# Second layer of a four-layer graph network: when K is put in place, when the bound is taken, and when the first tile of adj is fetched

## Chip, cores and metric

The kernel runs on one core of one Trainium2 chip. The metric is the device time of one execution in microseconds (us), median of several runs. One core has five engines with a queue of instructions each: TensorE (PE, matmuls), VectorE (DVE), ScalarE (ACT), GpSimd (POOL) and SyncE (SP). DMA transfers between SBUF, the on-chip memory, and DRAM are issued from the queues of SP, ACT and POOL. All sizes are float32.

## What is computed

Four graph layers run one after the other on x (4096 x 128) with one adjacency matrix adj (4096 x 4096, zeros and ones, symmetric); each is followed by a residual and a layer norm. The change touches the second one, a transformer convolution with 4 heads of 32 channels:

```python
def _transformer_conv(x, adj, Wq, bq, Wk, bk, Wv, bv, Ws, bs, Wb):
    q = (x @ Wq + bq).reshape(n, H, C)
    k = (x @ Wk + bk).reshape(n, H, C)
    v = (x @ Wv + bv).reshape(n, H, C)
    attn = jnp.einsum('nhc,mhc->hnm', q, k) / np.float32(np.sqrt(C))
    mask = adj == 0.0
    # softmax of attn over m where mask is false, called alpha
    out = jnp.einsum('hnm,mhc->hnc', alpha, v)
    out = jnp.transpose(out, (1, 2, 0)).reshape(n, C * H)
    x_r = x @ Ws + bs
    beta = jax.nn.sigmoid(jnp.concatenate([out, x_r, out - x_r], axis=-1) @ Wb)
    return beta * x_r + (1.0 - beta) * out
```

## The kernel before

The second layer has a prologue and a loop. The prologue computes q and k in 8 chunks of S = 512 nodes. Each chunk is cut into a rounded part and a remainder (`cut`), written to the DRAM tensor `qk`, and read back by `stack` into an arrangement in which one 128-row matmul gives the sum of the partial products of one head: `KS` holds all of k (4096 nodes), `QS[0]` and `QS[1]` hold one chunk of q each. The prologue also computes v (into `VA`) and x_r (written to the DRAM tensor `rd`), and a bound on the scores: if it is at most SAFE, the exponential needs no shift.

```python
KS = keep.tile([P, NH, N], F32R, tag="KS", name="KS")
QS = [keep.tile([P, NH, S], F32R, tag=f"QS{k}", name=f"QS{k}") for k in range(2)]
# ...
def stack(a, dst, c):                       # four transfers of 32 partitions
    for r, part in enumerate(((0, 1, 0, 1), (0, 0, 1, 1))[a]):
        nc.gpsimd.dma_start(
            out=dst[r * C : (r + 1) * C, :, :],
            in_=qk[a, part, :, c * S : (c + 1) * S].rearrange("(h c) n -> c h n", h=NH),
        )
# ...
for c in range(NC):                         # NC = 8
    s = slice(c * S, (c + 1) * S)
    for a, w, bias in ((1, wk, bkc), (0, wq, bqc)):
        p = self.ps_t.tile([P, S], F32, tag="pt", name="pqk")
        nc.tensor.matmul(p, lhsT=w, rhs=XT[:, s], start=True, stop=True)
        cut = rot.tile([P, 2, S], F32R, tag="cut", name="cut", bufs=4)
        nc.scalar.activation(cut[:, 0, :], p, AF.Identity, bias=bias)             # L820
        nc.vector.scalar_tensor_tensor(cut[:, 1, :], p, bias, ...)                # L821
        nc.vector.tensor_reduce(mx[:, a, c : c + 1], ..., ALU.max, ...)           # L824
        nc.sync.dma_start(out=qk[a, :, :, s].rearrange("k p n -> p k n"), in_=cut.bitcast(F32))
        if a:
            stack(1, KS[:, :, s], c)
        elif c < 2:
            stack(0, QS[c], c)
# the bound: m2 from mx, one matmul pb, a reduction, then fi = (bound <= SAFE)    # L833 to L843
for g in self.groups():                     # 8 groups of 4: v                    # L844
    # ... 4 matmuls pt <- XT, wv; 4 additions V[:, t, :, 0:C] = p + bvr           # L847, L849
for g in self.groups():                     # 8 groups of 4: x_r                  # L855
    # ... 4 matmuls pt <- XT, ws                                                  # L858
    r = rot.tile([P, 4, D], F32, tag="r", name="r")       # rot has 2 buffers
    nc.vector.tensor_tensor(r, p, bsr..., ALU.add)                                # L860
    nc.sync.dma_start(out=rd[:, g[0] : g[-1] + 1, :], in_=r)

small = nc.values_load(fi, min_val=0, max_val=1)
with tc.If(small > 0) as cmp:
    self.attention_unshifted(VA, KS, QS, stack, rd, wb)
with cmp.Else():
    self.attention_shifted(V, qk, rd, wb)
```

The loop (`attention_unshifted`, the branch that runs with these inputs) has 8 tiles I of 512 nodes with 32 steps jb each. A step forms the scores of 4 heads (`ps`), their exponentials (`e`), masks them with a piece of the transposed adj (`at`), and, two steps later, multiplies them into the sums (`pv`). Inside it the instructions keep the order in which they are written.

```python
atp = ctx.enter_context(tc.tile_pool(name="atf", bufs=2))
def load(I, J):                             # 1 MB of adjT, on SP's queue
    at = atp.tile([P, 4, S], F32, tag="at", name="at")
    nc.sync.dma_start(out=at, in_=self.adjT[I, J])                                # L884
    st["at", I, J] = at
# row(n): 1 MB of adj into nat, on ACT's queue (L894); degree(n): ACT sums nat (L901), then row(n + 1)
# scores(I, jb): ps <- KS, QS (L909); e = exp(ps) (L916); e *= (at != 0) (L918)
# sums(I, jb): pv <- VA, e (L935)

nc.scalar.preload_act_table_set("natural_log_exp_and_others")                     # L1006
load(0, 0)
load(0, 1)
row(0)
for n in range(-LEAD, len(seq)):            # LEAD = 2
    if n + LEAD < len(seq):
        I, jb = seq[n + LEAD]
        if jb % 4 == 0:
            m = n + LEAD + 4
            if m < len(seq) and (m // 4) > 1:
                load(m // NT, m % NT // 4)
        if jb % 4 == 3:
            degree(8 * I + jb // 4)
        if jb == 3 and 0 < I < NS - 1:
            stack(0, QS[(I + 1) % 2], I + 1)
        scores(I, jb)
    if n >= 0:
        sums(*seq[n])
        # ... and the ending of the tile before, in pieces
```

Of the kernel before, what the change touches and what calls it, by code (L numbers as in the profile page):

```python
# [16 lines left out]
P = 128  # L17
# [7 lines left out]
S = 512  # L25
# [5 lines left out]
class Net:  # L31
# [737 lines left out]
    def layer1(self, Wq, bq, Wk, bk, Wv, bv, Ws, bs, Wb):  # L769


        nc, tc, N, NT, D, X = self.nc, self.tc, self.N, self.NT, self.D, self.X
        NH, C = 4, D // 4
        with ExitStack() as ctx:
            self.on_scalar = 4
            keep = ctx.enter_context(tc.tile_pool(name="keep1", bufs=1))

            VA = keep.tile([P, NT * NH * (C + 1) + 32], F32, tag="VA", name="VA")
            V = VA[:, 0 : NT * NH * (C + 1)].rearrange("p (t h c) -> p t h c", t=NT, h=NH)
            KS = keep.tile([P, NH, N], F32R, tag="KS", name="KS")  # L780
            QS = [keep.tile([P, NH, S], F32R, tag=f"QS{k}", name=f"QS{k}") for k in range(2)]

            qk = self.dram.tile([2, 2, P, N], F32, tag="qk", name="qk")
            rd = self.dram.tile([P, NT, D], F32, tag="rd", name="rd")
            wb = [self.load_row(Wb[k * D : (k + 1) * D, 0], f"wb{k}") for k in range(3)]

            nc.vector.tensor_tensor(wb[0], wb[0], wb[2], ALU.add)
            nc.vector.tensor_tensor(wb[1], wb[1], wb[2], ALU.subtract)
            fi = self.const.tile([1, 1], mybir.dt.int32, tag="fi", name="fi")
            wq, wk = self.load_mat(Wq, "wq"), self.load_mat(Wk, "wk")  # L790
            wv, ws = self.load_mat(Wv, "wv"), self.load_mat(Ws, "ws")
            bqc, bkc = self.load_col(bq, "bqc"), self.load_col(bk, "bkc")
            bvr, bsr = self.load_row(bv, "bvr"), self.load_row(bs, "bsr")

            def stack(a, dst, c):
# [7 lines that stand above are left out]
            with ExitStack() as pctx:  # L803
                pre = pctx.enter_context(tc.tile_pool(name="pre1", bufs=1))
                rot = pctx.enter_context(tc.tile_pool(name="rot1", bufs=2))
                self.ps_t = pctx.enter_context(tc.tile_pool(name="ps_t", bufs=8, space=PSUM))
                nc.gpsimd.memset(VA, 1.0)
                XT = pre.tile([P, N], F32, tag="XT", name="XT")
                NC = N // S
                mx = pre.tile([P, 2, NC], F32, tag="mx", name="mx")  # L810
                self.transposed(X, XT)
                nc.vector.tensor_scalar(bqc, bqc, 1.0 / math.sqrt(C), None, op0=ALU.mult)
                nc.vector.tensor_scalar(wq, wq, 1.0 / math.sqrt(C), None, op0=ALU.mult)
                for c in range(NC):
                    s = slice(c * S, (c + 1) * S)
                    for a, w, bias in ((1, wk, bkc), (0, wq, bqc)):
                        p = self.ps_t.tile([P, S], F32, tag="pt", name="pqk")
                        nc.tensor.matmul(p, lhsT=w, rhs=XT[:, s], start=True, stop=True)
                        cut = rot.tile([P, 2, S], F32R, tag="cut", name="cut", bufs=4)
                        nc.scalar.activation(cut[:, 0, :], p, AF.Identity, bias=bias)  # L820
                        nc.vector.scalar_tensor_tensor(  # L821
                            cut[:, 1, :], p, bias, cut[:, 0, :].bitcast(F32), op0=ALU.add, op1=ALU.subtract
                        )
                        nc.vector.tensor_reduce(  # L824
                            mx[:, a, c : c + 1], cut[:, 0, :].bitcast(F32), AX.X, ALU.max, apply_absolute_value=True
                        )
                        nc.sync.dma_start(out=qk[a, :, :, s].rearrange("k p n -> p k n"), in_=cut.bitcast(F32))
                        if a:
                            stack(1, KS[:, :, s], c)
                        elif c < 2:  # L830
                            stack(0, QS[c], c)

                m2 = pre.tile([P, 2], F32, tag="m2", name="m2")  # L833
                nc.vector.tensor_reduce(m2, mx, AX.X, ALU.max)
                nc.vector.tensor_tensor(m2[:, 0:1], m2[:, 0:1], m2[:, 1:2], ALU.mult)
                hd = pre.tile([P, NH], F32, tag="hd", name="hd")
                nc.gpsimd.memset(hd, 0.0)
                for h in range(NH):
                    nc.gpsimd.memset(hd[h * C : (h + 1) * C, h : h + 1], 1.0)
                p = self.ps_t.tile([P, S], F32, tag="pt", name="pb")  # L840
                nc.tensor.matmul(p[0:1, 0:NH], lhsT=m2[:, 0:1], rhs=hd, start=True, stop=True)
                nc.vector.tensor_reduce(m2[0:1, 0:1], p[0:1, 0:NH], AX.X, ALU.max)
                nc.vector.tensor_scalar(fi, m2[0:1, 0:1], SAFE, None, op0=ALU.is_le)  # L843
                for g in self.groups():  # L844
                    p = self.ps_t.tile([P, 4, P], F32, tag="pt", name="pt")
                    for k, t in enumerate(g):
                        nc.tensor.matmul(p[:, k, :], lhsT=XT[:, t * P : (t + 1) * P], rhs=wv, start=True, stop=True)  # L847
                    for k, t in enumerate(g):
                        nc.vector.tensor_tensor(  # L849
                            V[:, t, :, 0:C],  # L850
                            p[:, k, :].rearrange("p (h c) -> p h c", h=NH),
                            bvr.rearrange("p (h c) -> p h c", h=NH),
                            ALU.add,
                        )
                for g in self.groups():  # L855
                    p = self.ps_t.tile([P, 4, P], F32, tag="pt", name="pt")
                    for k, t in enumerate(g):
                        nc.tensor.matmul(p[:, k, :], lhsT=XT[:, t * P : (t + 1) * P], rhs=ws, start=True, stop=True)  # L858
                    r = rot.tile([P, 4, D], F32, tag="r", name="r")
                    nc.vector.tensor_tensor(r, p, bsr.unsqueeze(1).to_broadcast([P, 4, D]), ALU.add)  # L860
                    nc.sync.dma_start(out=rd[:, g[0] : g[-1] + 1, :], in_=r)

            small = nc.values_load(fi, min_val=0, max_val=1)
            with tc.If(small > 0) as cmp:
                self.attention_unshifted(VA, KS, QS, stack, rd, wb)
            with cmp.Else():
                self.attention_shifted(V, qk, rd, wb)

    def attention_unshifted(self, VA, KS, QS, stack, rd, wb):

        nc, tc, N, NT, NS, D, X = self.nc, self.tc, self.N, self.NT, self.NS, self.D, self.X
        NH, C = 4, D // 4
# [1 line left out]
        with ExitStack() as ctx:  # L874
# [2 lines left out]
            ep = ctx.enter_context(tc.tile_pool(name="ef", bufs=3))  # L877
            ps_s = ctx.enter_context(tc.tile_pool(name="ps_s", bufs=3, space=PSUM))
            ps_v = ctx.enter_context(tc.tile_pool(name="ps_v", bufs=1, space=PSUM))
            st = {}  # L880

            def load(I, J):
                at = atp.tile([P, 4, S], F32, tag="at", name="at")
# [120 lines left out]
            rest = iter(())  # L1004
            with tc.manual_schedule():
                nc.scalar.preload_act_table_set("natural_log_exp_and_others")  # L1006
                load(0, 0)
                load(0, 1)
                row(0)
                for n in range(-LEAD, len(seq)):  # L1010
# [5 lines that stand above are left out]
                                load(m // NT, m % NT // 4)  # L1016
                        if jb % 4 == 3:
                            degree(8 * I + jb // 4)
                        if jb == 3 and 0 < I < NS - 1:
                            stack(0, QS[(I + 1) % 2], I + 1)  # L1020
                        scores(I, jb)
                    if n >= 0:
                        I, jb = seq[n]
                        sums(I, jb)
                        next(rest, None)
                        if jb == NT - 1:
                            for _ in rest:
                                pass
                            rest = ending(I)
                            next(rest)  # L1030
# [416 lines left out]
```

## Time and profile before

| | |
|---|---|
| time, median of 3 runs | 2433.75 us (2432.07 to 2436.35) |
| span of the profiled execution | 2429.7 us |
| mean granted TensorE clock | 0.913 |
| first matmul pqk of q and k | 979.5 us from the span's start |
| first matmul ps of the scores | 1049.8 us |
| first matmul pv of the sums | 1060.7 us |
| first tile of the loop (pv) | 1060.7 to 1157 us |
| end of the loop's matmuls | about 1873 us |

Times in the views count from the start of the span. A line of the chain of waits gives start, length and what the chain went through; "DMA qk<-cut" is a stretch in which the work that ended last stood waiting for that transfer. A line of busy time by windows gives the stretch, its length, the busy time of each engine with its instructions in brackets, the granted TensorE clock, the mean share of the 16 DMA engines (it can exceed 1) and the bytes moved per second. A line on a DMA queue gives packets, megabytes and the share of 16 engines; a line on DMA issues gives what is moved, the queue, how many, the size of one and the time from issue to landing. Line numbers (L918) are lines of the kernel before.

### The profile page before, as it was taken

The numbers are of one execution on the slowest core, as the hardware profiler recorded it, in microseconds if no ns is written. First come the engines' busy times: TensorE is split into PE (matmuls) and PEld (weight loads), VectorE is DVE, ScalarE is ACT, GpSimd is POOL, SyncE is SP. The second block draws the span as 40 slices with busy tenths as digits, with TensorE's granted clock in tenths as the row PEclk, the third lists the DMA queues.
The fourth block names the chain that finished last, engine by engine and source line by source line (L and its number), as shares of the span: only waits on it lengthen the run. The fifth ranks groups of instructions, "written<-read, shape, count | busy, mean of one in ns | idle before, by whom it ended". The sixth has DMA issues, their size and how long they took to land.

```text
span 2429.7 us, 24219 instructions
## 1 busy us (share of the span) xinstructions
PE 2016.8 (83%) x8795; PEld 1115.1 (46%) x8795; DVE 1902.7 (78%) x2719; ACT 1459.5 (60%) x1761; POOL 100.8 (4%) x141
## 2 busy tenths in 40 slices
PE   4477887788777771569999999999998799969998
PEld 4366666566656650333333333333333344444443
DVE  7478788788878888647877878787787887668887
ACT  5688888898888877247787777877776000010000
POOL 2000000000000051300000000000000000000000
PEclk7688989888898885689999999999999899989999
DMA  2455466465655630965564645646444788528784
GB/s 52 147 178 204 141 208 201 162 192 177 192 169 173 195 104 1 276 200 179 180 195 156 192 159 179 199 153 194 169 150 164 290 287 285 206 104 297 286 287 169
DMA packets 115175, 452.66 MB, mean 186 GB/s; under 512 B 10017, under 2 KB 20321, under 8 KB 74081
## 3 DMA queue, kind: packets, MB, share of 16 engines
q1 hardware_dynamic: 87392, 299.95, 36.6%
q10 hardware_dynamic: 18432, 134.23, 15.8%
q0 software_dynamic: 9216, 16.78, 3.5%
q8 instruction: 73, 1.20, 0.2%
q14 instruction: 62, 0.50, 0.1%
HBM read 371.20 MB, written 79.72 MB: 186 GB/s over the span
## 4 chain that ended last, share of the span: by engine, by line
PE 56%; DVE 24%; ACT 13%; DMA 3%; issue 3%; ACTq 0%; SPq 0%; POOL 0%; DVEq 0%; POOLq 0%
PE pv L935 14%; PE pa L1322 9%; PE pa L1177 9%; PE ps L909 8%; DVE e L918 5%; PE pz L583 4%; PE pi L674 3%; PE ptA L564 3%; DVE w L606 3%; DVE t L632 3%; DVE w L636 3%; ACT t L628 2%; ACT e L916 2%; ACT at L572 2%; ACT w L601 1%
## 5 line engine op out<-in xcount | busy, mean ns | idle before, releaser
L918 DVE SCALAR_TENSOR_TENSOR e<-at,e 128x2048 f32<-128x2048 f32 x256 | 581.2, 2287 | 171.2 <-ACT e L916 162.3
L916 ACT ACTIVATE e<-ps 128x1024 f32<-128x1024 f32 x512 | 489.3, 1025 | 162.4 <-PE ps L909 133.6
L935 PE MATMUL pv<-e,VA 128*64 128x512 f32 x2048 | 497.5, 607 | 12.6 <-DVE e L918 12.6
L909 PE MATMUL ps<-QS,KS 128*128 128x512 f32 x1024 | 314.6, 426 | 40.9 <-ACT e L916 27.5
L909 PEld LDWEIGHTS ps<-QS,KS 128*128 128x128 f32 x1024 | 171.5, 189 | 268.6 <-ACT e L916 171.3
L674 PE MATMUL pi<-HA,w 128*128 128x129 f32 x1152 | 184.8, 334 | 83.8 <-DVE w L636 83.8
L935 PEld LDWEIGHTS pv<-e,VA 128*64 128x64 f32 x2048 | 124.9, 136 | 255.1 <-issue 229.5
L1322 PE MATMUL pa<-w,F 128*128 128x512 f32 x512 | 223.2, 597 | 14.1 <-DVE w L1319 14.1
L1177 PE MATMUL pa<-at,Y 128*128 128x512 f32 x512 | 223.1, 596 | 0.0
L674 PEld LDWEIGHTS pi<-HA,w 128*128 128x128 f32 x1152 | 177.9, 247 | 94.0 <-DVE w L636 94.0
L1319 DVE SCALAR_TENSOR_TENSOR w<-rho,col,at 128x512 f32<-128x512 f32 x256 | 186.9, 748 | 18.8 <-PE pa L1322 1.6
L591 DVE SCALAR_TENSOR_TENSOR t<-ei,de,pz 128x512 f32<-128x512 f32 x144 | 107.5, 748 | 111.6 <-PE pz L583 107.9
L564 PE MATMUL ptA<-ident,ad 128*128 128x128 f32 x1032 | 146.5, 288 | 39.6 <-ACT at L572 32.5
L1187 DVE SCALAR_TENSOR_TENSOR odd<-at 128x2048 f32<-128x2048 f32 x64 | 146.6, 2291 | 37.9 <-DMA at<-adjT 37.4
L583 PE MATMUL pz<-HT 128*128 128x512 f32 x292 | 167.3, 685 | 4.2 <-DVE w L655 3.8
L564 PEld LDWEIGHTS ptA<-ident,ad 128*128 128x128 f32 x1032 | 125.4, 148 | 98.0 <-ACT at L572 50.1
L572 ACT COPY at<-ptA 128x512 f32<-128x512 f32 x200 | 108.5, 587 | 102.2 <-PE ptA L564 101.5
L1322 PEld LDWEIGHTS pa<-w,F 128*128 128x128 f32 x512 | 97.3, 192 | 135.0 <-issue 100.0
L1177 PEld LDWEIGHTS pa<-at,Y 128*128 128x128 f32 x512 | 97.5, 192 | 119.9 <-issue 118.7
L606 DVE TENSOR_TENSOR w<-w,at 128x2048 f32<-128x2048 f32 x64 | 143.8, 2283 | 0.0
L1326 ACT COPY a<-pa 128x512 f32<-128x512 f32 x8 | 4.7, 586 | 206.0 <-PE pa L1322 206.0
L642 PE MATMUL ptz<-ident,t 128*128 128x128 f32 x448 | 69.5, 297 | 67.2 <-DVE w L655 45.3
(340 smaller groups left out, 2426.5 us busy)
## 6 DMA issues: line engine op xcount, KB each, us to landing
at<-adjT SPq DMA_DIRECT2D x128, 1024.0 KB, 4.8
ad<-in_adj_dram SPq DMA_DIRECT2D x64, 1024.0 KB, 6.5
adjT<-at SPq DMA_DIRECT2D x64, 1024.0 KB, 8.3
nat<-in_adj_dram ACTq DMA_DIRECT2D x64, 1024.0 KB, 4.9
at<-adjT ACTq DMA_DIRECT2D x64, 1024.0 KB, 4.9
qk<-cut SPq DMA_DIRECT2D x16, 512.0 KB, 9.1
KS<-qk POOLq DMA_DIRECT2D x32, 256.0 KB, 11.0
QS<-qk POOLq DMA_DIRECT2D x32, 256.0 KB, 8.0
```

The costliest lines, as they stand in the source:

```text
L564: nc.tensor.transpose(pt[:, ib, :], st[p]["ad"][k][:, ib, jb * P : (jb + 1) * P], self.ident)
L572: copy(st[p]["at"][k][:, jb, :], st[p]["pt"].pop(m))
L583: nc.tensor.matmul(pz, lhsT=HT[:, j * P : (j + 1) * P], rhs=HT[:, I * S : (I + 1) * S], start=True, stop=True)
L606: nc.vector.tensor_tensor(w, w, at, ALU.mult)
L674: nc.tensor.matmul(self.po[ib // 2][:, ib % 2, :], lhsT=w[0][:, jb, ib * P : (ib + 1) * P], rhs=HA[:, 4 * J + jb, :], start=False, stop=(J ...
L909: nc.tensor.matmul(p[:, h, :], lhsT=KS[:, h2 + h, jb * P : (jb + 1) * P], rhs=QS[I % 2][:, h2 + h, :], start=True, stop=True,)
L916: nc.scalar.activation(e[:, h2 : h2 + 2, :], p, AF.Exp)
L918: nc.vector.scalar_tensor_tensor(e, at[:, jb % 4, :].unsqueeze(1).to_broadcast([P, NH, S]), 0.0, e, op0=ALU.not_equal, op1=ALU.mult,)
L935: nc.tensor.matmul(st["po"][h // 2][g : g + 64, :], lhsT=VA[:, o : o + 64], rhs=e[:, h, :], start=(jb == 0), stop=(jb == NT - 1), skip_gro ...
L1177: nc.tensor.matmul(pa, lhsT=Y[:, 4 * J + jb, :], rhs=at[:, jb, :], start=False, stop=(J == NS - 1 and jb == 3), skip_group_check=True,)
L1319: nc.vector.scalar_tensor_tensor(w, rho[:, I * S : (I + 1) * S], col[:, 0, j : j + 1], at[:, jb, :], op0=ALU.max, op1=ALU.mult)
L1322: nc.tensor.matmul(pa, lhsT=F[:, j, :], rhs=w, start=False, stop=(j == NT - 1), skip_group_check=True)
```

## The change

Three things are moved. **K:** the prologue reads back only the first two chunks of k into `KS`, as it does for q; the other six are read back in the loop's first tile, each two groups of four steps ahead of its use. **The bound:** its few instructions stand after v and x_r, as the last of the prologue. **The first tile of adj:** it has a buffer of its own (`at0`) that is filled at the beginning of the layer, on ACT's queue, ahead of the branch. Besides, `cut` has 9 buffers in place of 4, and `r` 4 in place of 2. Nothing that is computed changes. The change is meant to shorten the time between the last work of the first layer and the first steps of the loop, in which transfers are waited for.

```diff
--- before.py
+++ after.py
@@ -779,6 +779,8 @@
             V = VA[:, 0 : NT * NH * (C + 1)].rearrange("p (t h c) -> p t h c", t=NT, h=NH)
             KS = keep.tile([P, NH, N], F32R, tag="KS", name="KS")
             QS = [keep.tile([P, NH, S], F32R, tag=f"QS{k}", name=f"QS{k}") for k in range(2)]
+            at0 = keep.tile([P, 4, S], F32, tag="at0", name="at0")
+            nc.scalar.dma_start(out=at0, in_=self.adjT[0, 0])
 
             qk = self.dram.tile([2, 2, P, N], F32, tag="qk", name="qk")
             rd = self.dram.tile([P, NT, D], F32, tag="rd", name="rd")
@@ -816,7 +818,7 @@
                     for a, w, bias in ((1, wk, bkc), (0, wq, bqc)):
                         p = self.ps_t.tile([P, S], F32, tag="pt", name="pqk")
                         nc.tensor.matmul(p, lhsT=w, rhs=XT[:, s], start=True, stop=True)
-                        cut = rot.tile([P, 2, S], F32R, tag="cut", name="cut", bufs=4)
+                        cut = rot.tile([P, 2, S], F32R, tag="cut", name="cut", bufs=9)
                         nc.scalar.activation(cut[:, 0, :], p, AF.Identity, bias=bias)
                         nc.vector.scalar_tensor_tensor(
                             cut[:, 1, :], p, bias, cut[:, 0, :].bitcast(F32), op0=ALU.add, op1=ALU.subtract
@@ -825,22 +827,8 @@
                             mx[:, a, c : c + 1], cut[:, 0, :].bitcast(F32), AX.X, ALU.max, apply_absolute_value=True
                         )
                         nc.sync.dma_start(out=qk[a, :, :, s].rearrange("k p n -> p k n"), in_=cut.bitcast(F32))
-                        if a:
-                            stack(1, KS[:, :, s], c)
-                        elif c < 2:
-                            stack(0, QS[c], c)
-
-                m2 = pre.tile([P, 2], F32, tag="m2", name="m2")
-                nc.vector.tensor_reduce(m2, mx, AX.X, ALU.max)
-                nc.vector.tensor_tensor(m2[:, 0:1], m2[:, 0:1], m2[:, 1:2], ALU.mult)
-                hd = pre.tile([P, NH], F32, tag="hd", name="hd")
-                nc.gpsimd.memset(hd, 0.0)
-                for h in range(NH):
-                    nc.gpsimd.memset(hd[h * C : (h + 1) * C, h : h + 1], 1.0)
-                p = self.ps_t.tile([P, S], F32, tag="pt", name="pb")
-                nc.tensor.matmul(p[0:1, 0:NH], lhsT=m2[:, 0:1], rhs=hd, start=True, stop=True)
-                nc.vector.tensor_reduce(m2[0:1, 0:1], p[0:1, 0:NH], AX.X, ALU.max)
-                nc.vector.tensor_scalar(fi, m2[0:1, 0:1], SAFE, None, op0=ALU.is_le)
+                        if c < 2:
+                            stack(a, (QS[c], KS[:, :, s])[a], c)
                 for g in self.groups():
                     p = self.ps_t.tile([P, 4, P], F32, tag="pt", name="pt")
                     for k, t in enumerate(g):
@@ -856,17 +844,29 @@
                     p = self.ps_t.tile([P, 4, P], F32, tag="pt", name="pt")
                     for k, t in enumerate(g):
                         nc.tensor.matmul(p[:, k, :], lhsT=XT[:, t * P : (t + 1) * P], rhs=ws, start=True, stop=True)
-                    r = rot.tile([P, 4, D], F32, tag="r", name="r")
+                    r = rot.tile([P, 4, D], F32, tag="r", name="r", bufs=4)
                     nc.vector.tensor_tensor(r, p, bsr.unsqueeze(1).to_broadcast([P, 4, D]), ALU.add)
                     nc.sync.dma_start(out=rd[:, g[0] : g[-1] + 1, :], in_=r)
 
+                m2 = pre.tile([P, 2], F32, tag="m2", name="m2")
+                nc.vector.tensor_reduce(m2, mx, AX.X, ALU.max)
+                nc.vector.tensor_tensor(m2[:, 0:1], m2[:, 0:1], m2[:, 1:2], ALU.mult)
+                hd = pre.tile([P, NH], F32, tag="hd", name="hd")
+                nc.gpsimd.memset(hd, 0.0)
+                for h in range(NH):
+                    nc.gpsimd.memset(hd[h * C : (h + 1) * C, h : h + 1], 1.0)
+                p = self.ps_t.tile([P, S], F32, tag="pt", name="pb")
+                nc.tensor.matmul(p[0:1, 0:NH], lhsT=m2[:, 0:1], rhs=hd, start=True, stop=True)
+                nc.vector.tensor_reduce(m2[0:1, 0:1], p[0:1, 0:NH], AX.X, ALU.max)
+                nc.vector.tensor_scalar(fi, m2[0:1, 0:1], SAFE, None, op0=ALU.is_le)
+
             small = nc.values_load(fi, min_val=0, max_val=1)
             with tc.If(small > 0) as cmp:
-                self.attention_unshifted(VA, KS, QS, stack, rd, wb)
+                self.attention_unshifted(VA, KS, QS, at0, stack, rd, wb)
             with cmp.Else():
                 self.attention_shifted(V, qk, rd, wb)
 
-    def attention_unshifted(self, VA, KS, QS, stack, rd, wb):
+    def attention_unshifted(self, VA, KS, QS, at0, stack, rd, wb):
 
         nc, tc, N, NT, NS, D, X = self.nc, self.tc, self.N, self.NT, self.NS, self.D, self.X
         NH, C = 4, D // 4
@@ -877,7 +877,7 @@
             ep = ctx.enter_context(tc.tile_pool(name="ef", bufs=3))
             ps_s = ctx.enter_context(tc.tile_pool(name="ps_s", bufs=3, space=PSUM))
             ps_v = ctx.enter_context(tc.tile_pool(name="ps_v", bufs=1, space=PSUM))
-            st = {}
+            st = {("at", 0, 0): at0}
 
             def load(I, J):
                 at = atp.tile([P, 4, S], F32, tag="at", name="at")
@@ -1004,7 +1004,6 @@
             rest = iter(())
             with tc.manual_schedule():
                 nc.scalar.preload_act_table_set("natural_log_exp_and_others")
-                load(0, 0)
                 load(0, 1)
                 row(0)
                 for n in range(-LEAD, len(seq)):
@@ -1016,6 +1015,9 @@
                                 load(m // NT, m % NT // 4)
                         if jb % 4 == 3:
                             degree(8 * I + jb // 4)
+                        if I == 0 and jb % 4 == 0 and jb // 4 + 2 < NS:
+                            c = jb // 4 + 2
+                            stack(1, KS[:, :, c * S : (c + 1) * S], c)
                         if jb == 3 and 0 < I < NS - 1:
                             stack(0, QS[(I + 1) % 2], I + 1)
                         scores(I, jb)
```

## The prediction

> **What bounds the kernel now.** I read the page for the shape of the whole, then busy time by windows to find the stage that the change touches, then the chain of waits in that stage, then the DMA view for what is moved there. Busy time by windows, for the prologue of the second layer and the first two tiles of its loop:
>
> ```profile
> 979.00:1060.70 81.70, 39.94 (x178) 27.24 (x178) 36.60 (x78) 21.00 (x29) 21.98 (x40) 0.71 1.02 296
> 1060.70:1157.00 96.30, 96.26 (x378) 37.09 (x380) 72.28 (x32) 73.09 (x78) 2.18 (x4) 0.98 0.51 170
> 1157.00:1253.00 96.00, 91.21 (x368) 35.10 (x366) 77.38 (x84) 72.28 (x80) 0.41 (x1) 1.00 0.51 172
> ```
>
> In the 81.7 us of the prologue no compute engine is busy for even half of the time (PE 39.94, DVE 36.60, ACT 21.00), while the DMA engines are full (share 1.02, 296 GB/s). In the loop it is the reverse: PE is busy for 96.26 of 96.30 us, and the DMA engines for half. So the prologue is bound by transfers and the loop's first tile by PE, and what the change can gain is time in the prologue: 81.7 of 2433.75 us, of which something must remain. The chain of waits in this stage:
>
> ```profile
> 987.65 7.83 DMA qk<-cut
> ...
> 997.08 8.99 DMA qk<-cut
> ...
> 1007.67 9.12 DMA qk<-cut
> ...
> 1030.88 8.07 DMA rd<-r
> ...
> 1039.79 5.23 DMA rd<-r
> ...
> 1045.86 2.03 DMA rd<-r
> ...
> 1049.39 2.02 DMA rd<-r
> 1051.56 6.65 DMA at<-adjT
> 1058.34 2.30 DVE e L918
> 1060.74 3.68 PE pv L935 x8
> ```
>
> Three kinds of wait: for a free `cut` buffer (25.9 us in these three), for a free `r` buffer and then the landing of the last `r` (17.4), and for the first tile of adj (6.65, of which ACT's two exponentials hide a part). Each is a transfer that queues behind others. The DMA view of 986 to 1019 us says which:
>
> ```profile
> q1 hardware_dynamic: 3334, 6.44, 59.2%
> q0 software_dynamic: 3028, 5.53, 53.0%
> ...
> qk<-cut SPq DMA_DIRECT2D x14, 512.0 KB, 9.1
> KS<-qk POOLq DMA_DIRECT2D x20, 256.0 KB, 11.0
> QS<-qk POOLq DMA_DIRECT2D x8, 256.0 KB, 11.0
> ```
>
> SP's writes of `qk` (q1, 6.44 MB) and POOL's read-back (q0, 5.53 MB) share the engines about half and half, 363 GB/s together in that window and 381 to 382 between 998 and 1018. A 512 KB write lands 9.1 us after its issue although 0.52 MB at 380 GB/s would take 1.4.
>
> [...]
>
> **The change part by part.**
>
> K. Before, the prologue moves 16 writes of 512 KB (8.39 MB), 32 + 8 read-backs of 256 KB (8.39 and 2.10) and 8 `rd` writes of 256 KB (2.10): 20.97 MB. After it moves 8.39 + 2.10 + 2.10 + 2.10 = 14.7 MB; 24 read-backs, 6.29 MB, go. At 380 GB/s that is 55.2 against 38.6 us, a difference of 16.6. Before, the stage doesn't reach 380 to its end: from 1028 to 1036 us, with only read-backs in flight, it moves 218 GB/s, and the last `r` groups then wait one after the other. So from the first write (983.0) to the last landing (1051.4) it takes 68.4 us and not 55.2. That tail goes too, if the writes never wait.
>
> Buffers of `cut`. Unhindered, one cut takes DVE 0.748 + 0.675 us in busy time, and the starts at the beginning of the stage are 1.25 us apart (984.37, 985.63, 986.88); with 16 cuts from 982.2 that ends near 1002.5. While 16 read-backs of the first two chunks are in flight, I keep the landing times of before: write 3 (from 0) at 995.5, then one per 2.65 us, as ACT's restarts show (998.17, 1000.81, 1003.52). With 9 buffers cut 15 waits for write 6, at 1003.5; its last DVE work ends at about 1005.5, where it was 1018.96. 13.5 us earlier.
>
> v and x_r. 32 additions of 284 ns with their gaps took 0.89 us per group of 4: 8 groups, 7.1 us, to 1012.7. PE's matmuls for them (9.6 us for v) now don't stand behind the bound's matmul and lie beside the cuts. The first four `r` follow, 4 x 0.70, to 1015.5, without a wait because there are 4 buffers. The read-backs are through at about 1011 (16 x 256 KB at 190 GB/s from 986, and latency); by then 9 of the 16 writes have landed, and 7 are left: 7 x 0.524 MB / 380 GB/s = 9.7 us, to 1019.5. The `rd` writes are in the same queue behind them, 0.7 us each: `r` 4 to 7 start at 1020.2 to 1022.3, the last ends at 1023.0 and lands at 1025.0 (2.0 us, the 2.02 of the chain). So here too transfers set the end: 14.7 MB in 42 us.
>
> The bound comes last, 1.06 us on DVE and PE (1018.99 to 1020.05 before), then 0.66 us until ACT starts behind the branch (1020.71), then the table load of 1.28 us. Before, the table load lay hidden under the prologue; now it doesn't. 1023.0 + 1.1 + 0.7 + 1.3 = 1026.1; the issue of `nat` takes 0.4 more, and the first exponential starts at about 1026.7, where it was 1052.02. Cost of the move within that: about 1.7 us, since the landing of the last `r` would have allowed 1025.
>
> First tile of adj. Before, from the first exponential to the first pv it took 8.7 us (1052.02 to 1060.74), with DVE waiting for adj until 1058.34. After, with `at0` in place since about 980: two exponentials 1.9, one mask 2.3, 0.1 to PE, 4.3 us. That takes 4.4 us away.
>
> First pv at 1026.7 + 4.3 = 1031.0, against 1060.74: **29.7 us earlier**.
>
> Given back in the loop. Six K chunks are now read in the first tile: 24 x 256 KB, which POOL issues one after the other with nothing to wait for but its earlier transfers. The tile consumes a chunk each 4 steps, 12.0 us (PE's rhythm is 2.99 us a step). Beside them `at` and `nat` need 1.05 MB each per 12 us, 175 GB/s (170 in the window of before). K alone goes at 218 GB/s, so a chunk of 1.05 MB needs about 5 us, some 8 with the others beside it, and chunk 2 is needed only 8 steps in, some 18 us after its issue. At the very start three transfers of 1 MB and K compete; `nat`, needed after the third exponential, may come a little late, as it did (1.86 us of ACT's idle time before). I take 1 us.
>
> Sum: 29.7 - 1 = 28.7 us, **2433.75 - 28.7 = 2405 us**, a ratio of 0.988.
>
> **The rivals.**
>
> A false wait. `KS` is written in slices (all heads, one chunk) in the very tile that reads it. If a matmul on chunk 0 also waits for the transfers of chunk 2, or a transfer of chunk c + 2 for the matmuls before it, then each of the six chunks exposes a landing of 8 to 11 us: 50 to 65 us lost, 2433.75 - 30 + 57 = about 2460. Against it: pqk of the first chunk starts at 979.5 while the last piece of `XT` is written at 982.1, and the write of the second chunk of `qk` doesn't wait for the read-back of the first, which has the same interleaved shape. I give it 4%.
>
> Transfers move the wait into the loop. The bytes aren't saved, only moved, and the first 30 us of the tile carry 6.3 MB more. If `at` and `nat` land late several times, 3 to 10 us come back: 2408 to 2415. For it: 9.1 us landings in the prologue. Against it: about half of the loop's DMA capacity is idle (share 0.51), and each transfer has 12 us. 20%.
>
> The prologue shortens further. If the writes get a larger share with 9 in flight instead of 4, the cuts end at 1002.5 and only DVE and the bound stand: 1002.5 + 7.1 + 5.6 + 1.1 = 1016.3, and pv at 1024, 36 us earlier: 2398. 15%.
>
> ACT held up. The issue of `at0` stands in ACT's queue at the layer's beginning, and its buffer lies where the first layer had its own. If that isn't free, ACT, which is in the chain there (X L181), stops: 1 to 5 us. 15%.
>
> **Range and chances.** Middle 2405; 2397 if the writes gain share, 2412 if a few us come back in the loop or at ACT; a run of before itself spreads over 4.3 us. Range 2397 to 2412. Over 2% faster would need 48.7 us, more than the prologue holds beside its remaining transfers: 0.02. Over 2% slower needs the false wait in its full size: 0.03. Within 2%: 0.95.
>
> **What would show it.** Right: ACT's waits for `qk` nearly gone and the last cut near 1005; the first pv near 1031; 24 read-backs of K within the first tile; no DVE wait for the first `at`; 96 us for the first tile. Wrong: PE waiting for K, or DVE for `at`, in the first tile; ACT's first-layer work later than before; a first pv after 1040, which would mean that SP's writes and not the read-back held the prologue.

## The result, and the profile after

The changed kernel takes 2419.89 us (2417.39 to 2422.85), against 2433.06 for the kernel before beside it: a ratio of 0.9944 (95% interval 0.9927 to 0.9961). In a later repeat (g1 below) it was 0.9931 (0.9916 to 0.9945). It is faster, by some 13 to 17 us and not by the 28.7 that were predicted.

To read all runs alike, I cut each trace at three points: the first matmul of q and k (pqk), the first matmul of the sums (pv), and the last score matmul of the loop's first tile (it releases the first read-back of q in the loop, so its time stands in GpSimd's row). These stages don't depend on when the first layer ends, which moves by some us from run to run.

| us | first pqk to first pv | first pv to end of the first tile's scores | sum of the two |
|---|---|---|---|
| before | 81.2 | 89.4 | 170.6 |
| after | 54.1 | 99.3 | 153.4 |

The first stage lost 27.1 us, close to the prediction's 29.7. The second, which should have given back 1, gave back 9.9. The same in busy time by windows of the changed kernel, the two stages:

```profile
981.40:1035.50 54.10, 37.86 (x180) 25.39 (x179) 34.62 (x78) 18.13 (x26) 15.32 (x28) 0.82 1.00 305
1035.50:1134.80 99.30, 90.72 (x350) 34.26 (x352) 67.14 (x30) 70.10 (x74) 6.55 (x13) 0.94 0.80 215
```

In the second stage PE is idle for 8.6 us; in the kernel before it was busy throughout the first tile. The chain of waits of the changed kernel, from the first buffer wait on:

```profile
993.48 12.54 DMA qk<-cut
...
1008.18 6.33 DVE VA L837 x32
1014.51 0.61 DVE r L848
1015.14 7.73 DMA rd<-r
...
1023.58 0.05 DVE fi L861
1023.63 1.90 DVE r L848 x3
...
1025.55 4.97 DMA rd<-r
...
1030.62 15.52 DMA nat<-in_adj_dram
...
1048.19 12.34 DMA nat<-in_adj_dram
...
1062.59 10.68 DMA nat<-in_adj_dram
```

The three waits for `cut` have become one, the four for `r` two, and the one for the first tile of adj is gone. In its place stand three waits for `nat`, the rows of adj that ACT sums up beside the exponentials. Before, the median transfer of `nat` landed in 4.9 us and the longest in 7.9; here the first three take 15.5, 12.3 and 10.7. ACT takes its work in the order in which it is written: the score matmuls of the next step ended at 1041.8 us (1041.03 + 0.73), and their exponentials, behind the sum that waited for `nat`, began at 1048.63. DVE and PE waited with them. In order of time, after the third step:

```profile
1031.05 5.60 ACT L916 ACTIVATE e<-ps 128x1024 f32<-128x1024 f32 x6 [5.49 <-DMA rd<-r]
...
1041.03 0.73 PE L909 MATMUL ps<-QS,KS 128*128 128x512 f32 x2
...
1046.16 1.91 ACT L901 ACTIVATE nat<-nat 128x2048 f32<-128x2048 f32 x1 [9.50 <-DMA nat<-in_adj_dram]
...
1048.63 3.77 ACT L916 ACTIVATE e<-ps 128x1024 f32<-128x1024 f32 x4 [0.47 <-ACT nat L901]
...
1050.60 4.49 DVE L918 SCALAR_TENSOR_TENSOR e<-at,e 128x2048 f32<-128x2048 f32 x2 [10.82 <-ACT e L916]
```

ACT stood still for 9.50 us, and DVE behind it for 10.82. At the same time GpSimd had 24 read-backs of K to issue, and nothing but its own earlier transfers held it (16 waits, 24.3 us in sum). The DMA view of the changed kernel from 1030 to 1046 us, with the time to landing last:

```profile
q0 software_dynamic: 1034, 1.89, 73.5%
q1 hardware_dynamic: 229, 1.73, 34.3%
q10 hardware_dynamic: 144, 1.05, 18.3%
...
KS<-qk POOLq DMA_DIRECT2D x8, 256.0 KB, 19.0
at<-adjT SPq DMA_DIRECT2D x2, 1024.0 KB, 17.7
nat<-in_adj_dram ACTq DMA_DIRECT2D x1, 1024.0 KB, 15.5
```

K's packets (q0) take 73.5% of the engines' time for 1.89 MB, those of `nat` (q10) 18.3% for 1.05 MB. They do not run side by side. The same view from 1031 to 1036 us, when K, `at` and `nat` had all been issued, has one queue, and its first three from 1038 to 1044 are below that:

```profile
q0 software_dynamic: 593, 1.08, 154.3%
```

```profile
q1 hardware_dynamic: 141, 1.03, 49.3%
q10 hardware_dynamic: 126, 0.91, 42.1%
q0 software_dynamic: 140, 0.25, 13.2%
```

The busy time of these two stretches, and below it, for the kernel before, of the window in which only K was in flight:

```profile
1031.00:1036.00 5.00, 3.58 (x8) 1.82 (x10) 2.92 (x2) 4.95 (x6) 1.91 (x4) 0.50 1.54 217
1038.00:1044.00 6.00, 3.76 (x16) 1.45 (x14) 1.78 (x1) 0.00 (x0) 0.54 (x1) 0.98 1.06 369
```

```profile
1028.00:1036.00 8.00, 8.00 (x75) 8.00 (x74) 3.52 (x12) 0.00 (x0) 3.16 (x7) 1.00 1.53 218
```

The last number is GB/s. `at` and `nat` were issued at 1030.61 and 1030.62, and for more than 5 us nothing of them moved: K's queue had the engines to itself, at the 217 GB/s at which K runs alone. Then they moved, at 369 GB/s in sum, and K had little of it. So `nat` stood behind the read-backs of K that were queued ahead of it; what makes the queues take turns, no run here shows.

### The profile page after: what moved, and what is told of

It reads as the page before. It is cut to its first block, busy times and chain, and to the rows that moved or that the text cites. A ratio compares the mean times of both kernels' runs of the same rounds, so it can differ in the third digit from the quotient of the medians.

```text
span 2421.0 us, 24184 instructions
## 1 busy us (share of the span) xinstructions
PE 2028.3 (84%) x8795; PEld 1117.9 (46%) x8795; DVE 1900.7 (79%) x2719; ACT 1459.7 (60%) x1761; POOL 100.7 (4%) x141
## 4 chain that ended last, share of the span: by engine, by line
PE 56%; DVE 25%; ACT 12%; DMA 3%; issue 3%; ACTq 0%; SPq 0%; POOL 0%; DVEq 0%; POOLq 0%
PE pv L935 14%; PE pa L1324 9%; PE pa L1179 9%; PE ps L909 8%; DVE e L918 5%; PE pz L583 4%; DVE w L606 3%; PE pi L674 3%; DVE t L632 3%; DVE w L636 3%; PE ptA L564 3%; ACT t L628 3%; ACT at L572 2%; ACT e L916 2%; DMA nat<-in_adj_dram 2%
## 5 line engine op out<-in xcount | busy, mean ns | idle before, releaser
L935 PE MATMUL pv<-e,VA 128*64 128x512 f32 x2048 | 505.9, 616 | 7.8 <-DVE e L918 7.5
L1324 PE MATMUL pa<-w,F 128*128 128x512 f32 x512 | 224.0, 598 | 13.3 <-DVE w L1321 13.3
L901 ACT ACTIVATE nat<-nat 128x2048 f32<-128x2048 f32 x64 | 122.7, 1918 | 11.1 <-DMA nat<-in_adj_dram 11.1
## 6 DMA issues: line engine op xcount, KB each, us to landing
qk<-cut SPq DMA_DIRECT2D x16, 512.0 KB, 13.3
KS<-qk POOLq DMA_DIRECT2D x32, 256.0 KB, 11.1
```

Of the source, the lines that this page charges most:

```text
L935: nc.tensor.matmul(st["po"][h // 2][g : g + 64, :], lhsT=VA[:, o : o + 64], rhs=e[:, h, :], start=(jb == 0), stop=(jb == NT - 1), skip_gro ...
L1324: nc.tensor.matmul(pa, lhsT=F[:, j, :], rhs=w, start=False, stop=(j == NT - 1), skip_group_check=True)
```

## The experiments

**Theory:** the burst of 24 read-backs at the loop's start delays `nat`, and ACT's order turns the delay into lost steps. **Rivals:** three transfers of 1 MB at the branch are slow by themselves; or PE and DVE wait for K and `at`, and ACT's wait only stands in front of that. All edits are to the changed kernel unless said otherwise. The measured numbers, of all runs:

| run | pqk to pv | first tile | time, us | ratio to before (95%) |
|---|---|---|---|---|
| change | 54.1 | 99.3 | 2419.89 | 0.9944 (0.9927 to 0.9961) |
| change again (g1) | 54.5 | 99.9 | 2418.41 | 0.9931 (0.9916 to 0.9945) |
| e1, all of K in the prologue | 67.6 | 88.5 | 2421.11 | 0.9956 (0.9945 to 0.9967) |
| e2, nat from the second tile | 54.3 | 87.8 | 2418.58 | 0.9940 (0.9921 to 0.9959) |
| e3, K paced | 51.8 | 88.1 | 2400.67 | 0.9870 (0.9841 to 0.9898) |
| K paced again (g2) | 51.4 | 88.6 | 2404.73 | 0.9878 (0.9858 to 0.9897) |
| e4, K to 128 partitions | 54.0 | 93.9 | 2407.69 | 0.9906 (0.9880 to 0.9933) |
| g4, one wait, then the burst | 51.2 | 98.4 | 2412.77 | 0.9908 (0.9889 to 0.9928) |
| e5, bound early | 67.2 | 91.8 | 2420.26 | 0.9946 (0.9935 to 0.9956) |
| e6, no at0 | 65.7 | 89.1 | 2421.81 | 0.9956 (0.9937 to 0.9975) |
| e7, cut 4 and r 2 | 75.8 | 97.3 | 2436.29 | 1.0019 (1.0010 to 1.0028) |
| f1, K paced, second q late | 48.5 | 88.3 | 2401.24 | 0.9877 (0.9853 to 0.9900) |
| f1 again (g3) | 48.7 | 88.4 | 2402.17 | 0.9861 (0.9844 to 0.9879) |

**e1: K back in the prologue.**

```diff
-                        if c < 2:
-                            stack(a, (QS[c], KS[:, :, s])[a], c)
+                        if a:
+                            stack(1, KS[:, :, s], c)
+                        elif c < 2:
+                            stack(0, QS[c], c)
 # and the six read-backs in the first tile are taken out
```

> All of k is read back in the prologue again; the later bound, the early first tile of adj and the larger numbers of buffers stay. Theory (the burst of 24 read-backs of K at the loop's start delays the transfer of nat, and ACT, which takes its work in order, stops for it): ACT's idle time before nat in the first tile falls from 11.1 us to under 3, the first tile (first pv to the read-back of the third chunk of q) from 99.3 to about 90 us; but the prologue moves 21 MB again and the first pv comes about 8 us later than with the change: 2416 to 2424 us. Rival (three transfers of 1 MB started together at the branch are slow by themselves, K or no K): nat is still waited for by about 10 us, and with the longer prologue the time is 2427 to 2430.

ACT's wait for `nat` fell to 1.8 us and the first tile to 88.5: the first rival falls, since the three transfers of 1 MB still start together (`nat` landed in 7.84). The first stage grew by 13.5 us, more than the 8 expected, the first tile shrank by 10.8, and the time is that of the change. So **the move of K, the first part of the change, brings next to nothing as it is made** (156.1 - 153.4 = 2.7 us in the two stages, and nothing that the times show); the other parts without it give 170.6 - 156.1 = 14.5 us.

**e2: nat out of the first tile.**

```diff
-                        if jb % 4 == 3:
-                            degree(8 * I + jb // 4)
+                        k = n + LEAD - NT
+                        if k == -8:
+                            row(0)
+                        if k >= 0 and k % 3 == 2 and k // 3 < len(halves):
+                            degree(k // 3)
```

> The row sums of adj (nat) begin in the second tile, one per three steps instead of one per four, so that no nat is moved in the first tile; K is read back in the first tile as in the change. Theory: all of ACT's long waits in the first tile were for nat; the first tile takes about 90 us instead of 99, later tiles stay as they are, and the time is 9 to 11 us below the change's 2419.9: about 2410. Rival (the tile is slow because PE or DVE wait for K or at, and ACT's wait only stands in front of that): the wait moves to PE or DVE and the time stays within 3 us of 2420.

The first tile took 87.8 us with the burst of K still in it: the second rival falls too, neither K nor `at` was late. (Without `nat` they also had fewer bytes beside them; e3 has all three.) The time, though, is 2418.58 and not 2410: the expectation that later tiles stay as they are was wrong. From the end of the first tile's scores to the loop's last score matmul it took 734.4 us, and 716.9 before. The same 64 sums stand closer together there. By GpSimd's row, four of the next five tiles take 106.2 to 109.1 us, where those of the change take 102.8 to 104.2; the cause stays open.

**e3: one chunk of K per four steps.**

```diff
-                        if I == 0 and jb % 4 == 0 and jb // 4 + 2 < NS:
+                        if I == 0 and jb % 4 == 1 and jb // 4 + 2 < NS:
                             c = jb // 4 + 2
+                            nc.gpsimd.tensor_copy(tick, st["e", 0, jb - 1][:, 0, 0:1])
                             stack(1, KS[:, :, c * S : (c + 1) * S], c)
```

> As the change, but GpSimd waits, ahead of the read-back of chunk c + 2, for the masked exponentials of step 4c (a copy of one column), so that one chunk of K is in flight per four steps instead of all six at once. Theory: the last write of rd lands in about 2 us again instead of 5, nat in 6 to 9 us instead of 15.5, 12.3 and 10.7, ACT's wait for nat falls under 2 us: 2408 to 2412 us. Rival (three transfers of 1 MB together are slow by themselves): the first nat still takes over 12 us, and the time is 2416 to 2420.

Better than expected: 2400.67 us, ACT's wait for `nat` 1.5 us in the whole loop, the first tile at 88.1. The chain of waits between 1018 and 1100 us of this kernel has three transfers, and no `nat` after the first:

```profile
1010.48 7.55 DMA rd<-r
1020.72 2.10 DMA rd<-r
1022.93 7.52 DMA nat<-in_adj_dram
```

The last write of `rd` lands in 2.10 us where it took 4.97, because GpSimd no longer starts the burst while it is under way (its first read-back in the loop goes out at 1029.88 us, after that landing at 1022.82; in the change at 1024.84, before the one at 1030.52); with that the first stage is 51.8, the prediction's 51.5. Against e1, which differs in where and how K is read, the two stages are 156.1 - 139.9 = 16.2 us shorter: paced, the move of K is worth about the 16.6 us that the prediction worked out from its bytes (the medians, on one chip, lie 20.4 apart). Windows of two later groups of four steps:

```profile
1042.00:1054.00 12.00, 12.00 (x51) 4.64 (x48) 9.08 (x4) 9.66 (x11) 4.42 (x6) 1.00 1.04 260
1054.00:1066.00 12.00, 12.00 (x52) 4.64 (x48) 9.08 (x4) 9.56 (x11) 4.44 (x6) 1.00 1.04 263
```

PE is busy for 12.00 of 12.00 us while K, `at` and `nat`, about 1 MB each, move at 260 GB/s on the average. They take turns here too (from 1043 to 1047 us K's queue alone moves anything, 0.89 MB), but with four read-backs queued, and not all, no `nat` of this kernel takes more than 9.7 us to land, and a group has 12. The bytes of K fit beside the loop; all at once they don't.

**g4: one wait, then the burst.** The same edit as e3, but the copy into `tick` is made for the first of the six chunks only.

> As the paced version, but GpSimd waits once only, for the first masked exponentials, and then issues all 24 read-backs of K one after the other. If it is the meeting of the burst with the last rd writes and the first nat that costs (the start): the first nat lands in under 10 us, the later ones have a step's slack, ACT waits under 3 us, the first tile takes 88 to 90 us, the time is within 3 us of the paced version. [...]

This separates the two things that pacing changed. The first stage is as short as with pacing (51.2), so the delay of the last `rd` was the meeting at the start. The first tile is as long as in the change (98.4), where 88 to 90 were expected if that meeting were the cost:

```profile
1023.03 7.81 DMA nat<-in_adj_dram
...
1032.89 12.33 DMA nat<-in_adj_dram
...
1047.27 11.53 DMA nat<-in_adj_dram
...
1060.86 13.27 DMA nat<-in_adj_dram
```

The first `nat`, ahead of the burst, lands in 7.81; the next three, beside it, in 11.5 to 13.3, and a group of four steps is 12.0. So what costs is the burst itself, which here begins at 1029.98 us, after the landing of the last `rd` (1022.93), and not its meeting with the start. The time is 8.0 us above the paced version on the same chip.

**e4: the shape of K's transfers.**

```diff
-                            stack(1, KS[:, :, c * S : (c + 1) * S], c)
+                            for h in range(NH):
+                                nc.gpsimd.dma_start(
+                                    out=KS[:, h, c * S : (c + 1) * S], in_=qk[1, h // 2, :, c * S : (c + 1) * S]
+                                )
```

> In the loop's first tile K is read by transfers of 128 partitions x 2 KB instead of 32 partitions x 4 x 2 KB: as many, as large, from the same queue, but the wrong parts of k for six of the eight chunks (the arrangement is left out). [...] Theory B (GpSimd's issue or the bytes themselves set the pace): K stays at about 170 to 220 GB/s, nat takes 13 to 16 us, and the time is 2417 to 2421.

This kernel leaves out the arrangement of six chunks of K; bytes, number and queue of the transfers are those of the change. Its windows in the burst, first with K's queue alone at work, then with `at` and `nat` moving:

```profile
1025.00:1028.00 3.00, 1.56 (x4) 1.01 (x4) 0.60 (x1) 2.63 (x3) 2.05 (x5) 0.50 1.25 389
1029.00:1035.00 6.00, 5.70 (x22) 1.90 (x20) 5.10 (x3) 1.97 (x3) 1.09 (x3) 0.81 1.05 415
```

Theory B falls: K alone moves at 389 GB/s, where the change had 217, so that what is queued ahead of `nat` is gone sooner. The first `nat` lands in 10.6 us instead of 15.5, ACT waits 4.5 instead of 11.1, and the tile takes 93.9. So about half of the loss in the tile, 5.4 of 9.9 us, comes from the 32-partition shape, and the rest from the burst as such. That the shape sets K's rate, 217 or 389 GB/s, e4 shows; why it does, no run here shows.

**e5: the bound where it was.** The bound's block is moved back ahead of v and x_r.

> As the change, but the bound stands ahead of v and x_r again, where it was. Theory (the late bound's worth is that it holds GpSimd, and so the burst of K, behind the prologue's last writes): GpSimd passes the branch some 15 us earlier, right after the bound, the burst of K meets the writes of qk and rd, and the first pv comes 60 to 66 us after the first pqk instead of 54.1; the first tile, with less of K left, takes 90 to 95 us instead of 99.3; the time is 2418 to 2426 us. Rival (the place of the bound matters only by its own instructions, about 1.7 us): 52 to 54 us to the first pv, 99 for the first tile, 2416 to 2420.

67.2 and 91.8 us, nearly as the theory had it. GpSimd's row shows why:

```profile
1010.45 3.75 POOL L800 DMA_DIRECT2D KS<-qk  x7 [6.19 <-issue]
```

It begins the burst at 1010.45 (29.0 us after the first pqk; 43.4 in the change), ahead of the first write of `rd` (1019.85). DVE then waits 10.8 us for `rd` instead of 5.2. So the bound's place matters mainly as a gate for what stands behind the branch on other queues. It is not all: v's matmuls stand behind the bound's matmul again, and DVE starts v at 1010.93, 2.8 us after its last cut, where in the change there was no gap. The two stages are 5.6 us longer than the change's in this one profile; the median is 2420.26 and can't tell that from the change (the runs of e5 lie between 2417.11 and 2426.24).

**e6: no at0.** The first tile of adj is fetched by `load(0, 0)` at the loop's start again.

> As the change, but the first tile of adj is fetched in the loop as before, and has no buffer of its own. Prediction's size for this part: 4.4 us. Theory (in the change this transfer would meet the burst of K as nat does): its landing takes 10 to 15 us from the branch, the first pv comes 60 to 65 us after the first pqk instead of 54.1, but nat is waited for in the same time, so that the first tile takes 4 to 8 us less; the time is 2 to 6 us above the change.

65.7 and 89.1, sum 154.8 against 153.4: DVE waits 19.2 us for `at`, and ACT's 8.5 us for `nat` lie beside that. Beside the burst, `at0` exchanges one wait for another: the first tile is 10.2 us shorter, more than the 4 to 8 expected. It is worth 1.4 us in the stages, not 4.4, and as the change itself had 153.4 and 154.4 in its two traces, even that may be nothing.

**e7: buffers as before.** `cut` bufs 9 to 4, `r` bufs 4 to 2.

> As the change, but cut has 4 buffers and r 2, as before. Theory (the larger numbers let the cuts run ahead of the writes): ACT waits for qk in sum over 15 us instead of 6.9, the last cut comes 7 us later, DVE waits for rd more than once; the first pv comes 60 to 64 us after the first pqk instead of 54.1, and the time is 2425 to 2430 us. Rival (the transfers set the end of the prologue in any case, and the buffers only shift where one waits): 54 to 57 us, and 2420 to 2423.

Worse than either theory: 75.8 us, 2436.29, slower than the kernel before. ACT waits 18.8 us for `qk`, as expected. What was not expected is the tail. With two buffers the bound gets done after the second `r` (at 1025.18), GpSimd begins its burst, and the last four `r` go out one by one beside it; three of them:

```profile
1026.53 4.27 POOL L800 DMA_DIRECT2D KS<-qk  x8 [26.49 <-DVE r L848]
...
1031.71 0.69 DVE L848 TENSOR_TENSOR r<-pt,bsr 128x512 f32<-128x512 f32 x1 [2.64 <-DMA rd<-r]
...
1037.10 0.69 DVE L848 TENSOR_TENSOR r<-pt,bsr 128x512 f32<-128x512 f32 x1 [4.70 <-DMA rd<-r]
...
1040.24 0.69 DVE L848 TENSOR_TENSOR r<-pt,bsr 128x512 f32<-128x512 f32 x1 [2.45 <-DMA rd<-r]
```

The part of the change that is not one of its three moves carries it: with the buffers as before, the three bring nothing. `cut` and `r` were taken back together here, and the buffers alone, without the three moves, were not run.

**f1: paced, and the second chunk of q late.** To e3 it adds:

```diff
-                        if c < 2:
+                        if (a, c) in ((1, 0), (1, 1), (0, 0)):
                             stack(a, (QS[c], KS[:, :, s])[a], c)
# and in the first tile, at jb == 25, the same kind of copy into tick, then stack(0, QS[1], 1)
```

> As the paced version e3, and the second chunk of q, which is used in the second tile alone, is read back in the last quarter of the first tile instead of in the prologue. Theory (the end of the prologue is set by its bytes, 14.7 MB, the last of them in the queue behind the writes of qk): 1.05 MB less takes 2.8 us off at 380 GB/s, and up to 5 where the read-back ran at 190 GB/s beside the writes; the first pv 47 to 49 us after the first pqk instead of 51.8, the first tile 88 us as in e3, the time 2396 to 2398 us. Rival (DVE's chain of cuts, v and x_r sets the end): the first pv stays within 1 us of 51.8, the time at 2400.

The prologue got 3.3 us shorter, as the theory of bytes has it. The time didn't show it: 2401.24 against 2400.67.

**Repeats on one chip.**

> The change itself once more, beside the next three on the same chip: 2417 to 2423 us, the first pv 54 us after the first pqk, the first tile 99 us, ACT waiting 9 to 12 us for nat.

> The paced version e3 once more, on the same chip as the change: 52 and 88 us for the two stages, 13 us less than the change in them (153.4 against 139.9), so 12 to 20 us less in the whole: 2400 to 2408.

> The version f1 (paced, the second chunk of q late) once more: if the 3.3 us that the prologue loses come through, it is 2 to 4 us below the paced version; if the later tiles give them back, as the one trace of f1 has it, the two are within 1.5 us.

The change 2418.41, paced 2404.73, with the second q late 2402.17. Pacing is worth 13.7 us over the change here. The late q is 2.6 us below that, but the two intervals overlap: it is not settled. Both versions are faster than the change and than the kernel before, at 0.986 to 0.988.

## Why the prediction was wrong, step by step

**What bounds the kernel: right.** The prologue was bound by transfers, the tile by PE.

**The prologue: right in mechanism and nearly in size.** Predicted 51.5 us from the first pqk to the first pv, measured 54.1, and 51.8 once the burst doesn't meet the last `rd`. The terms: the last cut's DVE work ends 26.0 us after the first pqk (1005.5 - 979.5), measured 26.8 (1008.18 - 981.4); v and x_r's first four came as worked out. The missed term is the landing of the last `rd`: 2.0 us assumed, from a row in which nothing else was in flight, 4.97 measured, because the same bound that opens the branch for ACT opens it for GpSimd. That e3's 51.8 comes so close to 51.5 is partly luck: its last `rd` goes out 44.7 us after the first pqk (1020.72 - 976.0), where 43.5 was predicted by a sum that is 1.2 short (1011 and 9.7 make 1020.7, not 1019.5); against that, the bound's cost behind it, 1.7, is not there.

**The bound: mis-read.** It was priced by its own instructions and the table load, 1.7 us, as the last things done. In the change its last instruction (`fi` in the chain) was done at 1023.63, ahead of the last three additions of `r`, so all of this lay under the landing of the last `rd` and cost nothing. e5 shows its real effect: the place of the bound sets when the burst begins.

**at0: right alone, not in company.** 4.4 us predicted; 1.4 in e6, since the wait for `nat` takes its place.

**The step that failed: "Given back in the loop ... I take 1 us".** It measured 9.9. The sum of bytes behind it was sound, as e3 shows: 260 GB/s, and PE without a gap. Three things were wrong in how it was used. First, it spread K over the tile, a chunk per 12.0 us, although the same paragraph says that GpSimd "issues one after the other with nothing to wait for but its earlier transfers". Second, it let K and the wide transfers move side by side (a chunk in "some 8 with the others beside it"), and took a loop whose engines are half idle on the average as one with room at every moment. The traces show turns: `nat`, issued at 1030.62, moved nothing before 1036, while K ahead of it went at 217 GB/s. Third, it looked at whether K comes in time (it does, PE never waits for it) and not at whose transfer has the least slack beside K: `nat`, with one buffer, one group of four steps, and an engine that works in order behind it.

**The rivals.** The false wait didn't come: no score matmul of the first tile waits for K. "Transfers move the wait into the loop" is what happened, put at 20% and at 3 to 10 us; it came to 9.9 in the tile and 2.6 in the prologue. That the prologue shortens further, to a first pv 36 us earlier, did not come: 27.1. Nor was ACT held up by the issue of `at0`: the first pqk starts at 981.4 us in the change and at 978.1 in its repeat, against 979.5 before. The stages account for 153.4 - 170.6 = -17.2 us; the medians say -13.2 and, in the repeat, -16.9. The profiled execution of the change was also 3.3 us longer than before in the later tiles and 3.3 in the last layers; in the repeat's trace these are 0.4 and 2.5. I take that for spread, since no part of the change lies there.

## What to carry to other kernels

A transfer moved off the critical path is not gone: ask which queue will issue it, what holds that queue, and which transfer already there has the least slack and an in-order engine behind it. Here a one-column copy that makes the issuing engine wait for the loop, one chunk at a time, was worth 13.7 us on top of the change's 16.9 (2435.29 - 2418.41, the same chip). And where a barrier such as a branch is moved, look at every queue that it releases, not only at the one that was waited for.

## What the runs showed of the hardware that was not expected

- A wide transfer issued on one queue behind a number of read-backs on another stood still until most of these were gone. `nat` and `at`, issued at 1030.6, moved nothing from 1031 to 1036 us while K's queue moved 1.08 MB; a 1 MB `nat` that takes 4.9 us in the steady loop took 15.5. With K to 128 partitions the same happened, only shorter, as K went at 389 GB/s and not at 217: 10.6. An average such as 260 GB/s can so hide that the queues take turns.
- The same narrow read-backs beside writes in the other direction did not take turns but shared the engines about half and half (3.70 and 3.91 MB, 56.1% and 58.6% of their time), and came to 381 GB/s together (998 to 1018 us of the kernel before), where the read-backs alone made 218.
- GpSimd's copy of one column into `tick` looks slow, about 2.3 us (2279 ns median of six in e3), but in f1 and g3, which pace K in the same way, one of six took 183 ns. The long ones end with the mask on DVE that ran beside them (below, from e3, the last of three masks at 1034.99 + 6.70 = 1041.69 and the copy at 1039.61 + 2.11 = 1041.72), so as far as these traces go the copy waits for the mask. GpSimd's issuing does not: e3's first four read-backs of K go out 0.54 us apart from 1029.88 to 1032.02, beside a mask that ends at 1032.09. The copy is off the path here.

```profile
1034.99 6.70 DVE L919 SCALAR_TENSOR_TENSOR e<-at,e 128x2048 f32<-128x2048 f32 x3 [2.90 <-ACT e L917]
...
1039.61 2.11 POOL L1021 COPY tick<-e 128x1 f32<-128x1 f32 x1 [7.59 <-DVE e L919]
```
